# Spacing the typed masks of a graph transformer's second layer in a planned instruction order

## The chip, the cores and the metric

The kernel runs on one core of a Trainium2 chip. The metric is the device time of one execution in microseconds (us). The engines are named as in the profile: PE (TensorE matmul) and PEld (its weight loads), DVE (VectorE), ACT (ScalarE), POOL (GpSimd), SP (SyncE, which here only issues transfers).

## The reference

Two layers of an attention network over a graph with 6250 nodes of 128 values, 200000 edges sorted by destination, 32 edge types, 16 node types and 8 heads; then a linear map, the input added, and a layer norm. What matters of one layer:

```
k, q, v = typed_linear(x, ntype, Wk), ...Wq, ...Wv    # one 128x128 matrix per node type
a   = sum(kT[src, type] * q[dst]) per head            # kT, vT: k and v through one small matrix per edge type
att = softmax of a over the edges of one dst
hag = segment_sum(vT[src, type] * att, dst)
h   = silu(typed_linear(hag, ntype, Wa)) * alpha + x * (1 - alpha)
x   = layer_norm(h) * g + b
```

`typed_linear` multiplies each node's row by the matrix of that node's type. The kernel does it for a group of nodes with 16 masks: mask t holds the transposed rows with all columns zeroed that are not of type t, and 16 matmuls, one per type, add up in one PSUM bank.

## The kernel before

**Stages.** A preparation sorts the nodes by degree and builds, for layer 1, a table in DRAM with one row (key and value, 256 floats) per node and edge type. Each layer then gathers table rows: 49 tiles of 128 nodes, each tile with as many slots as its largest degree needs (1604 slots in all). One gather (line 921, POOL) brings one slot, a row for each of 128 nodes, into a ring buffer in SBUF. In layer 1 the ring has 64 slots, in layer 2 it has 96 (`RINGS`). A gather into a used slot waits until DVE has freed that slot. Layer 1 also builds layer 2's table; layer 2, which the change touches, has gathers, attention and output work only.

**Attention of one tile** (`attend_part`, DVE, in pieces of up to 16 slots): keys times query (L961), sum per head (L963), after all pieces the maximum and the difference (L967 to L972), the exponential on ACT (L974), its sum (L977 to L980), then for each piece values times weights (L988) and their sum (L992). L992 frees the piece's slots.

**Output work of a group** (`behind` and `head`). Tiles form 15 groups: ten of 4 tiles, then groups of 3, 2, 2, 1 and 1. When a group's last tile is done, its sums (`hag`) are transposed on PE; then come 16 masks on DVE (L1072) and 16 matmuls on PE (L1080, tile `av` or `tab`, weights `wa`); one copy on ACT (L1087, `yT`); a transpose back; tanh, skip connection, layer norm, final linear map and second norm; and one scatter per tile on POOL (L1224). In layer 2, two groups can be at this work at once, on two pairs of PSUM banks (`lanes`), taken in turn by a lock that each group gives back near its end.

**Query rows** (`early_rows`, layer 2). One thread goes through groups 2 to 14, loads their layer-1 output from DRAM (`xq`, `tq`), transposes, makes 16 masks and 16 matmuls (weights `wq`), copies (L1087, `qT`), transposes, copies again (`q`) and writes the rows to DRAM, from where a group's tiles fetch them later. It may run any number of groups ahead of the attention.

**Masks.** Both users go through `typed_cols` (L1063). Its `mask` thread makes mask t as soon as the mask buffer is free: with 8 buffers in layer 2 (`XML`), mask t waits for the matmul of mask t-8. The two users share the tag `xm`, so on the chip the 8 buffers go round over the masks of both.

**What sets the order.** `Plan` writes out the order of all instructions before the launch. Every thread yields an engine, a duration and what it needs; `Plan.run` always takes the step that can start first by its own clock; among steps that can start at the same time the lower rank goes first. The ranks here are 1.4 for the masks of the output work ("masks"), 1.6 for attention, 1.8 for the masks of query rows ("early"). On the chip only the order counts: each engine works through its list in that order and waits at an instruction until its semaphores allow it. `LAGS` says that in layer 2 the plan takes the result of any PE work as known 20 us after its end, while gathers run. Scatters are put into POOL's order up to 130 us (`LATE`) after the plan has the rows.

Of the kernel before, what the change touches and what calls it, by code (L numbers as in the profile page):

```python
# [38 lines left out]
P = 128  # L39
# [5 lines left out]
GT = 4  # L45
# [15 lines left out]
XML = (4, 8)  # L61
LAGS = (0.0, 20.0)
XS = (4, 3)
LATE = 130.0
TAB = 512
QUAD = 1.22
GS = 4
# [141 lines left out]
def dve_us(n):  # L209
    return 0.15 + n / 960  # L210


def act_us(n):
    return 0.14 + n / 1200
# [18 lines left out]
def gnn_kernel(ctx: ExitStack, tc: tile.TileContext, x, src, dst, etype, ntype, Wk, Wq, Wv, Wa,  # L233
# [69 lines left out]
    early = ExitStack()  # L303
# [106 lines left out]
    def transposed(t, rows, n, needs):  # L410
        us = yield "PE", Work(n * P), needs
        for j in range(n):
            nc.tensor.transpose(t[:, j * P : (j + 1) * P], rows[:, j], ident)  # L413
        return t, us
# [42 lines left out]
    def table_rows(banks, st, kT, vT, j, bk, bv, needs, free):  # L457

        nodes = slice(j * P, (j + 1) * P)
        width = 2 * HS  # L460
        per = TAB // width
        assert 2 * per == RT
# [3 lines left out]
        for t0 in range(0, RT, per):  # L466
            i = 2 * t0 // RT
            for kv, (cT, blk) in enumerate(((kT, bk), (vT, bv))):
                for g0 in range(0, rows, quad):
                    us = yield "PE", Work(TAB, QUAD if quad > 1 else width / P), [*needs, *emptied[-len(banks):][:quad]]  # L470
                    for g in range(g0, g0 + quad):
# [9 lines left out]
                        def empty(to=st[i][:, :, c0 : c0 + width], tab=tab, done=done, us=us, i=i):  # L481
                            done.us, e = yield ("ACT", "DVE"), (act_us(TAB), dve_us(TAB)), [us, free[i]]
                            (nc.scalar.copy if e == "ACT" else nc.vector.tensor_copy)(  # L483
                                to, tab.rearrange("p (t o) -> p t o", o=width))
# [431 lines left out]
    NG = len(LAST)  # L916
    wqs = []
# [142 lines left out]
            nc.vector.tensor_scalar(low[:, :, 0], low[:, :, 0], float(ROUND), None, op0=ALU.add)  # L1060
            nc.vector.tensor_scalar(low[:, :, 1], low[:, :, 1], float(-ROUND), None, op0=ALU.add)

    def typed_cols(fp, xm_bufs, xT, types, M, maps, needs, rank="masks"):  # L1063

        ready, busy = [When() for _ in range(NT)], [When() for _ in range(NT)]
        masks = {}

        def mask():
            for t in range(NT):
                us = yield "DVE", dve_us(M), [*needs, busy[t - xm_bufs] if t >= xm_bufs else 0.0]  # L1070
                xm = fp.tile([P, GT * P], F32, tag="xm", name="xm", bufs=xm_bufs)
                nc.vector.scalar_tensor_tensor(xm[:, :M], types[:, :M], float(t), xT[:, :M], op0=ALU.is_equal, op1=ALU.mult)  # L1072
                masks[t], ready[t].us = xm, us

        plan.spawn(mask(), RANK[rank])
        for t in range(NT):
            busy[t].us = yield "PE", Work(M * len(maps)), [ready[t]]
            xm = masks.pop(t)
            for w, to in maps:
                nc.tensor.matmul(to[:, :M], w[:, t], xm[:, :M], start=(t == 0), stop=(t == NT - 1))  # L1080
        return busy[-1].us

    def copied4(fp, tag, acc, M, needs, bufs=1):
        us, e = yield ("ACT", "DVE"), (act_us(M), dve_us(M)), needs
        t = fp.tile([P, GT * P], F32, tag=tag, name=tag, bufs=bufs)
        if e == "ACT":
            nc.scalar.copy(t[:, :M], acc[:, :M])  # L1087
        else:
            nc.vector.tensor_copy(t[:, :M], acc[:, :M])
        return t, us  # L1090

    def turned(t, cT, n, needs):
        us = yield "PE", Work(n * P), needs
        for j in range(n):
            nc.tensor.transpose(t[:, j * P : (j + 1) * P], cT[:, j * P : (j + 1) * P], ident)
        return us

    def norm(fp, h, n, bufs=1):
        us = yield "DVE", n * 0.55, ()
        mv = fp.tile([P, GT, 2], F32, tag="mv", name="mv", bufs=bufs)  # L1100
        for j in range(n):
            bst = fp.tile([P, 6], F32, tag="bst", name="bst", bufs=2)
            nc.vector.bn_stats(bst, h[:, j])  # L1103
            nc.vector.bn_aggr(mv[:, j], bst)
        us = yield "ACT", 1.6, [us]
        rs = fp.tile([P, GT], F32, tag="rs", name="rs", bufs=bufs)
        nc.scalar.activation(rs[:, :n], mv[:, :n, 1], AF.Sqrt, bias=eps)  # L1107
        us = yield "DVE", 0.2 + n * dve_us(P), [us]
        nc.vector.reciprocal(rs[:, :n], rs[:, :n])
        for j in range(n):  # L1110
            nc.vector.tensor_scalar(h[:, j], h[:, j], mv[:, j, 0:1], rs[:, j : j + 1], op0=ALU.subtract, op1=ALU.mult)  # L1111
        return us

    def load4(fp, tag, ap, t0, n, bufs):
        t = fp.tile([P, GT, P], F32, tag=tag, name=tag, bufs=bufs)
        nc.sync.dma_start(out=t[:, :n], in_=ap[t0 * P : (t0 + n) * P].rearrange("(j p) d -> p j d", p=P))
        return t

    def behind(fp, layer, i, hag, fetched, needs, weights, wa, at):

        g = LAST[i]
        t0, n = g[0], len(g)
        M = n * P
        lane = lanes[layer * (1 + i % 2)]
        xb, acc, lock = lane
        turn = lock.take()
        xs, types, got = fetched
        xT, us = yield from transposed(xb, hag, n, [*needs, turn])
        at["hag"][i].us = us
        us = yield from typed_cols(fp, XML[layer], xT, types, M, [(wa, acc)], [us, got])  # L1130
        yT, us = yield from copied4(fp, "yT", acc, M, [us], 1 + layer)
        us = yield from turned(xb, yT, n, [us])
        y3 = xb.rearrange("p (j m) -> p j m", j=GT)[:, :n]
        us = yield "ACT", act_us(M) + 1.28, [us] + ([at["h"][i - 1 - layer]] if i > layer else [])
        h = fp.tile([P, GT, P], F32, tag="h", name="h", bufs=1 + layer)[:, :n]
        nc.scalar.activation(h, y3, AF.Tanh, scale=0.5)
        us = yield "DVE", dve_us(M), [us]
        nc.vector.scalar_tensor_tensor(h, h, 1.0, y3, op0=ALU.add, op1=ALU.mult)
        for j, t in enumerate(g):
            xs_us = yield "ACT", 0.3, [got]  # L1140
            nc.scalar.activation(xs[:, j], xs[:, j], AF.Copy, scale=beta[layer][:, t : t + 1])
            us = yield "DVE", dve_us(P), [us, xs_us]
            nc.vector.scalar_tensor_tensor(h[:, j], h[:, j], alpha[layer][:, t : t + 1], xs[:, j], op0=ALU.mult, op1=ALU.add)
        yield from norm(fp, h, n, 1 + layer)
        yield "DVE", dve_us(M), ()
        nc.vector.tensor_tensor(h, h, g_bc[layer][:, None, :].to_broadcast([P, n, P]), op=ALU.mult)  # L1146
        us = yield "DVE", dve_us(M), ()
        nc.vector.tensor_tensor(h, h, b_bc[layer][:, None, :].to_broadcast([P, n, P]), op=ALU.add)  # L1148
        if layer == L - 1:
            yield from head(fp, i, h, lane, [us], at)  # L1150
        else:
            yield from project(fp, i, h, types, weights, [us], at)
# [46 lines left out]
    def head(fp, i, h, lane, needs, at):  # L1199
# [20 lines left out]
        us = yield from norm(fp, o, n, 2)  # L1220
        us = max(us + 1.3, min(us + LATE, at["end"]))
        for j, t in enumerate(g):
# [35 lines left out]
    def attends(fp, layer, ring, pieces, st, weights, wa, pool, landed, freed):  # L1258
# [13 lines left out]
        came = {c: When() for c in ("wq", "wa", "next")}  # L1272
# [55 lines left out]
        def early_rows():  # L1328

            xb, acc, _ = lanes[3]  # L1330
            free, sent = [0.0, 0.0], [0.0, 0.0]
            for i, g in list(enumerate(LAST))[2:]:
                n = len(g)
                got = yield "SP", 0.9, [free[-2]]
                xs = load4(fp, "xq", hid, g[0], n, 1)
                types = fp.tile([P, GT * P], F32, tag="tq", name="tq", bufs=2)
                nc.sync.dma_start(out=types[:, : n * P],
                                  in_=tyrow[ds(g[0] * P, n * P)][None, :].to_broadcast([P, n * P]))
                xT, us = yield from transposed(xb, xs, n, [got + 3.0])
                us = yield from typed_cols(fp, XML[layer], xT, types, n * P, [(wqs[layer], acc)], [us, came["wq"]], "early")  # L1340
                free.append(us)
                qT, us = yield from copied4(fp, "qT", acc, n * P, [us])
                us = yield from turned(xb, qT, n, [us])
                q, us = yield from copied4(fp, "q", xb, n * P, [us, sent[-1]])
                us = yield "SP", 0.4, [us]
                nc.sync.dma_start(out=qrows[g[0] * P : (g[0] + n) * P].rearrange("(j p) d -> p j d", p=P),
                                  in_=q.rearrange("p (j d) -> p j d", d=P)[:, :n])
                sent.append(us + 2.5)
                asked[i].us = us + 2.5
# [20 lines left out]
        for i, g in enumerate(LAST):  # L1370
            if i > 2:
                yield "SP", 0.0, [at["hag"][i - 3]]
            n = len(g)
            hag = fp.tile([P, GT, P], F32, tag="hag", name="hag", bufs=3)
            for j, t in enumerate(g):
# [15 lines left out]
                us = yield "DVE", 0.4 + dve_us(P), ()  # L1391
# [7 lines left out]
    for layer in range(L):  # L1399
        last = layer == L - 1  # L1400
        with tc.tile_pool(name=f"wp{layer}", bufs=1) as wp, tc.tile_pool(name=f"fp{layer}", bufs=1) as fp, \
# [8 lines left out]
            wa = typed_tile(wp, "wa")  # L1410
# [147 lines left out]
```

## Time and profile before

| | |
|---|---|
| median of 3 runs | 6419.52 us (6408.02 to 6420.96) |
| profiled execution | 6422.69 us, its span 6420.9 us |
| busy in the span | PE 2871.1 us, DVE 3917.8 us, ACT 935.9 us, POOL 3427.8 us |
| granted TensorE clock, mean of the span | 0.649 |
| gathers (L921) | 3208, one 1000 ns busy |
| masks of both layers (L1072) | 880, one 589 ns in the mean of all widths |

A row of a list of instructions in order of time reads: start, duration, engine, line, operation, output and inputs, shape, how many were merged, and in brackets the engine's idle time before it with what ended that. "remote" and "issue" as releasers mean that the profile has no instruction of the program at that moment whose end explains the wait.

### The profile page before, as it was taken

What the parts mean: (1) busy time and instruction counts of PE and PEld (TensorE: products, weight loads), DVE (VectorE), ACT (ScalarE), POOL (GpSimd) and SP (SyncE); (2) the same over time, 40 slices, a digit from 0 to 9 for tenths busy, and PEclk for the clock granted to TensorE, in tenths of its full rate; (3) what the DMA queues carried; (4) which work ended last, traced back from release to release, by engine and by line L of the source; (5) the groups of instructions that cost most, each with busy time, mean ns of one, the idle gap of its engine ahead of it and who ended that gap; (6) DMA issues with size and microseconds to landing.
All of it is one profiled execution on the core that took longest, in us unless ns stands there. A gap on an engine that the chain in (4) does not pass through costs nothing. (4 is left out here: it accounts for less than half of the span.)

```text
span 6420.9 us, 36014 instructions
## 1 busy us (share of the span) xinstructions
PE 2871.1 (45%) x8591; PEld 1387.5 (22%) x8599; DVE 3917.8 (61%) x5664; ACT 935.9 (15%) x1921; POOL 3427.8 (53%) x3428
## 2 busy tenths in 40 slices
PE   5887941354555545655655664122232222221112
PEld 4553520121222212221222232010011111110002
DVE  7864637456555655565565563656466666666667
ACT  0333310020211202211111232000000000000001
POOL 4022036555546556555554524766676666767662
PEclk8998975566665566666666776565565565555555
DMA  4696873252525525434444544433333333333331
GB/s 118 264 388 252 338 262 87 74 179 75 186 90 168 178 79 188 168 104 158 157 128 150 181 171 178 117 89 103 103 104 93 98 97 97 99 104 99 94 97 34
DMA packets 323165, 923.16 MB, mean 144 GB/s; under 512 B 82759, under 2 KB 169844, under 8 KB 285312
## 3 DMA queue, kind: packets, MB, share of 16 engines
q0 software_dynamic: 161888, 438.75, 23.6%
q1 hardware_dynamic: 161056, 482.05, 19.9%
q8 instruction: 68, 1.11, 0.1%
q14 instruction: 153, 1.25, 0.1%
HBM read 486.99 MB, written 433.57 MB: 143 GB/s over the span
## 5 line engine op out<-in xcount | busy, mean ns | idle before, releaser
L921 POOL DMA_INDIRECT ring<-table,idx_all x3208 | 3208.5, 1000 | 2498.5 <-issue 2000.9
L1072 DVE SCALAR_TENSOR_TENSOR xm<-types,xb 128x512 f32<-128x512 f32 (+3 forms) x880 | 490.5, 589 | 665.9 <-remote 317.3
L483 ACT COPY st<-tab 128x512 f32<-128x512 f32 x1146 | 613.2, 597 | 1123.6 <-PE tab L474 532.8
L992 DVE TENSOR_REDUCE add<-ring 128x128 f32<-128x2048 f32 (+11 forms) x270 | 745.4, 2761 | 48.4 <-remote 28.6
L474 PE MATMUL tab<-bv,vT 32*128 32x512 f32 x1568 | 478.2, 797 | 172.5 <-issue 89.1
L474 PE MATMUL tab<-bk,kT 32*128 32x512 f32 x1568 | 455.2, 795 | 212.5 <-issue 159.6
L961 DVE TENSOR_TENSOR ring<-ring,sb 128x2048 f32<-128x2048 f32 (+12 forms) x266 | 459.9, 1729 | 143.0 <-DMA ring<-table,idx_all 126.5
L963 DVE TENSOR_REDUCE sb<-ring 128x128 f32<-128x2048 f32 (+11 forms) x270 | 470.7, 1743 | 58.1 <-remote 41.5
L483 DVE COPY st<-tab 128x512 f32<-128x512 f32 x422 | 275.1, 686 | 349.5 <-PE tab L474 176.9
L1080 PE MATMUL av<-xm,wa 128*128 128x512 f32 (+3 forms) x736 | 358.2, 641 | 273.3 <-DVE xm L1072 214.2
L1080 PE MATMUL tab<-xm,wq 128*128 128x512 f32 (+3 forms) x416 | 250.2, 755 | 508.9 <-DVE xm L1072 177.4
L988 DVE TENSOR_TENSOR ring<-ring,sb 128x2048 f32<-128x2048 f32 (+11 forms) x270 | 467.4, 1731 | 0.0
L1080 PE MATMUL av<-xm,wq 128*128 128x512 f32 (+3 forms) x544 | 285.6, 670 | 266.5 <-DVE xm L1072 215.9
L1080 PE MATMUL ak<-xm,wk 128*128 128x512 f32 (+3 forms) x480 | 247.2, 601 | 108.7 <-DVE xm L1072 91.0
L441 PE MATMUL kv<-xm,wk 128*128 128x256 f32 (+1 forms) x800 | 268.1, 419 | 43.4 <-DVE xm L426 42.8
L1234 ACT COPY sb<-qr 128x128 f32<-128x128 f32 x97 | 26.3, 271 | 1691.6 <-DVE sb L963 988.5
L1080 PEld LDWEIGHTS av<-xm,wa 128*128 128x128 f32 x736 | 155.3, 234 | 468.6 <-DVE xm L1072 272.0
L474 PEld LDWEIGHTS tab<-bv,vT 32*128 32x128 f32 x1568 | 170.5, 222 | 373.4 <-issue 178.9
L441 PE MATMUL kv<-xm,wv 128*128 128x256 f32 (+1 forms) x800 | 248.7, 394 | 0.0
L1080 PEld LDWEIGHTS tab<-xm,wq 128*128 128x128 f32 x416 | 105.7, 285 | 642.9 <-DVE xm L1072 217.5
L474 PEld LDWEIGHTS tab<-bk,kT 32*128 32x128 f32 x1568 | 158.6, 221 | 394.8 <-issue 249.9
L1080 PE MATMUL av<-xm,wv 128*128 128x512 f32 (+3 forms) x480 | 234.3, 573 | 0.0
(216 smaller groups left out, 2875.8 us busy)
## 6 DMA issues: line engine op xcount, KB each, us to landing
table<-st SPq DMA_DIRECT2D x196, 1028.0 KB
table<-st SPq DMA_DIRECT2D x98, 2048.0 KB
ring<-table,idx_all POOLq DMA_INDIRECT x3208
state<-init SPq DMA_DIRECT2D x2, 3528.0 KB
state<-state SPq DMA_DIRECT2D x98, 72.0 KB
types<-tyrow SPq DMA_DIRECT2D x20, 256.0 KB
rows<-in_x_dram SPq DMA_DIRECT2D x24, 128.0 KB
types_i<-in_node_type_dram SPq DMA_DIRECT2D x24, 128.0 KB
```

What stands on the lines that cost most here:

```text
L441: nc.tensor.matmul(to, w[:, t], xm, start=False, stop=last_of)
L474: nc.tensor.matmul(tab, cT[here, nodes], blk[here, t0 : t0 + per].rearrange("p t o -> p (t o)"), start=True, stop=True)
L483: (nc.scalar.copy if e == "ACT" else nc.vector.tensor_copy)(to, tab.rearrange("p (t o) -> p t o", o=width))
L921: nc.gpsimd.indirect_dma_start(out=ring[:, place], out_offset=None, in_=tables[layer], in_offset=bass.IndirectOffsetOnAxis(ap=idx[:, s : s ...
L961: nc.vector.tensor_tensor(kk, kk, q[:, None, :].to_broadcast([P, m, P]), op=ALU.mult)
L963: nc.vector.tensor_reduce(sc[:, s0 : s0 + m], kk.rearrange("p s (h d) -> p s h d", h=H), axis=AX.X, op=ALU.add)
L988: nc.vector.tensor_tensor(vv.rearrange("p s (h d) -> p s h d", h=H), vv.rearrange("p s (h d) -> p s h d", h=H), sc[:, s0 : s0 + m, :, None ...
L992: nc.vector.tensor_reduce(add, vv.rearrange("p s c -> p c s"), axis=AX.X, op=ALU.add)
L1072: nc.vector.scalar_tensor_tensor(xm[:, :M], types[:, :M], float(t), xT[:, :M], op0=ALU.is_equal, op1=ALU.mult)
L1080: nc.tensor.matmul(to[:, :M], w[:, t], xm[:, :M], start=(t == 0), stop=(t == NT - 1))
L1234: nc.scalar.copy(q, rows[0][:, j])
```

## The change

`typed_cols` takes one more argument, `pace`. The `mask` thread remembers the planned end of the mask before (`us`) and asks, as one more need, that mask t starts no earlier than `us + pace`. The output work passes `PACE * n / GT` in layer 2 for all but the last three groups (n tiles in the group, GT = 4), else 0. The query rows pass it for every group. `PACE` is 5.5 us: masks of a group of 4 tiles are planned 5.5 us apart from end to start, of 3 tiles 4.125, of 2 tiles 2.75, of 1 tile 1.375. The instructions, their number and their operands stay; their order on the engines' lists may change. Layer 1 passes no pace.

```diff
+PACE = 5.5
...
-    def typed_cols(fp, xm_bufs, xT, types, M, maps, needs, rank="masks"):
+    def typed_cols(fp, xm_bufs, xT, types, M, maps, needs, rank="masks", pace=0.0):
...
         def mask():
+            us = -pace
             for t in range(NT):
-                us = yield "DVE", dve_us(M), [*needs, busy[t - xm_bufs] if t >= xm_bufs else 0.0]
+                us = yield "DVE", dve_us(M), [*needs, us + pace, busy[t - xm_bufs] if t >= xm_bufs else 0.0]
...
-        us = yield from typed_cols(fp, XML[layer], xT, types, M, [(wa, acc)], [us, got])
+        us = yield from typed_cols(fp, XML[layer], xT, types, M, [(wa, acc)], [us, got], "masks",
+                                   PACE * n / GT if layer and i < NG - 3 else 0.0)
...
-                us = yield from typed_cols(fp, XML[layer], xT, types, n * P, [(wqs[layer], acc)], [us, came["wq"]], "early")
+                us = yield from typed_cols(fp, XML[layer], xT, types, n * P, [(wqs[layer], acc)], [us, came["wq"]], "early", PACE * n / GT)
```

## Rows read from the trace of the kernel before

**Rows 1.** Busy time by stretch: from layer 2's first gather to its last, then after.
```profile
3926.00:6294.00 2368.00, 552.41 (x1072) 244.60 (x1072) 1481.80 (x1874) 129.44 (x254) 1641.74 (x1640) 0.57 0.34 101
6294.00:6421.00 127.00, 37.63 (x152) 28.77 (x151) 99.28 (x227) 23.19 (x44) 12.93 (x14) 0.59 0.05 16
```

**Rows 2.** Instructions in order of time, POOL: an undisturbed gather of layer 2.
```profile
4022.13 1.00 POOL L921 DMA_INDIRECT ring<-table,idx_all  x1 [0.30 <-issue]
```

**Rows 3.** Who waited for whom, POOL, 3926 to 6421: total us, times, longest.
```profile
POOL ring L921 <- DVE add L992: 165.0, 16, 17.8
POOL out_dram L1224 <- DVE o L1111: 94.7, 4, 50.6
POOL ring L921 <- DVE rs L1109: 11.7, 1, 11.7
```

**Rows 4.** Groups of masks in layer 2 by shape: busy, mean ns, idle before.
```profile
L1072 DVE SCALAR_TENSOR_TENSOR xm<-tq,tab 128x512 f32<-128x512 f32 x128 | 80.0, 680 | 47.6 <-remote 31.5 <-issue 12.5 <-PE tab L1080 3.6
L1072 DVE SCALAR_TENSOR_TENSOR xm<-types,tab 128x512 f32<-128x512 f32 x80 | 50.6, 682 | 70.3 <-remote 40.3 <-issue 16.6 <-PE tab L1080 13.4
L1072 DVE SCALAR_TENSOR_TENSOR xm<-types,xb 128x512 f32<-128x512 f32 x80 | 50.0, 681 | 33.0 <-remote 23.9 <-issue 5.1 <-PE av L1080 4.0
L1072 DVE SCALAR_TENSOR_TENSOR xm<-tq,tab 128x256 f32<-128x256 f32 x32 | 11.6, 416 | 30.4 <-remote 28.7 <-PE tab L1080 1.7
```

**Rows 5.** DVE in order of time: masks of group 0's output work.
```profile
4227.66 4.87 DVE L1072 SCALAR_TENSOR_TENSOR xm<-types,xb 128x512 f32<-128x512 f32 x8
...
4265.72 0.69 DVE L1072 SCALAR_TENSOR_TENSOR xm<-types,xb 128x512 f32<-128x512 f32 x1 [4.91 <-issue]
4271.32 0.69 DVE L1072 SCALAR_TENSOR_TENSOR xm<-types,xb 128x512 f32<-128x512 f32 x1 [4.91 <-remote]
```

**Rows 6.** PE in order of time: that group's products; two matmul records make one.
```profile
4228.40 8.97 PE L1080 MATMUL av<-xm,wa 128*128 128x512 f32 x16 [12.04 <-issue]
...
4266.46 2.08 PE L1080 MATMUL av<-xm,wa 128*128 128x512 f32 x2 [4.47 <-DVE xm L1072]
```

**Rows 7.** PE in order of time: second half of the first query products.
```profile
3974.45 9.64 PE L1080 MATMUL tab<-xm,wq 128*128 128x512 f32 x16 [10.95 <-issue]
```

**Rows 8.** ACT in order of time: two copies of finished products.
```profile
4014.59 0.59 ACT L1087 COPY qT<-tab 128x512 f32<-128x512 f32 x1 [73.29 <-remote]
...
4594.24 0.58 ACT L1087 COPY yT<-tab 128x512 f32<-128x512 f32 x1 [35.29 <-remote]
```

**Rows 9.** DVE in order of time: the step after an exponential.
```profile
4595.18 0.47 DVE L977 TENSOR_REDUCE den<-sb 128x8 f32<-128x296 f32 x1 [34.48 <-ACT sb L974]
```

**Rows 10.** POOL in order of time: seven gathers that waited for the ring.
```profile
4664.69 0.99 POOL L921 DMA_INDIRECT ring<-table,idx_all  x1 [13.09 <-DVE add L992]
...
4822.25 1.00 POOL L921 DMA_INDIRECT ring<-table,idx_all  x1 [10.45 <-DVE add L992]
...
4884.04 0.99 POOL L921 DMA_INDIRECT ring<-table,idx_all  x1 [14.79 <-DVE add L992]
...
5045.81 0.99 POOL L921 DMA_INDIRECT ring<-table,idx_all  x1 [17.46 <-DVE add L992]
...
5297.00 1.00 POOL L921 DMA_INDIRECT ring<-table,idx_all  x1 [15.55 <-DVE add L992]
...
5446.36 1.00 POOL L921 DMA_INDIRECT ring<-table,idx_all  x1 [17.83 <-DVE add L992]
...
5724.26 1.00 POOL L921 DMA_INDIRECT ring<-table,idx_all  x1 [13.21 <-DVE add L992]
```

**Rows 11.** All masks of query rows in layer 2: ns min/median/max, first and last start.
```profile
L1072 DVE SCALAR_TENSOR_TENSOR xm<-tq,tab x208: 277/678/689, 3953.0 to 5871.8; 128x512 f32<-128x512 f32 x64, 128x256 f32<-128x256 f32 x16, 128x128 f32<-128x128 f32 x16, 128x384 f32<-128x384 f32 x8
```

**Rows 12.** DVE in order of time: first and last masks of group 10's output work.
```profile
6222.65 3.80 DVE L1072 SCALAR_TENSOR_TENSOR xm<-types,xb 128x384 f32<-128x384 f32 x8
...
6246.76 0.99 DVE L1072 SCALAR_TENSOR_TENSOR xm<-types,xb 128x384 f32<-128x384 f32 x2
```

**Rows 13.** DVE in order of time: masks soon after a wait for the ring.
```profile
5600.99 3.18 DVE L1072 SCALAR_TENSOR_TENSOR xm<-types,xb 128x512 f32<-128x512 f32 x5
```

## The prediction

> **What bounds the kernel now.** Read first the busy time by stretch, cut at layer 2's first and last gather [rows 1]: the change passes no pace in layer 1, so nothing before moves. In those 2368 us POOL issues 1640 transfers (1604 gathers, 36 scatters). One takes 1.00 us busy and 0.30 us before the next [rows 2]; 1640 x 1.30 = 2132 us is what gathering alone would need. So 236 us are waiting. The waits by pair come next [rows 3]: 165.0 + 11.7 = 176.7 us of them are gathers that wait for a ring slot that DVE has not freed. The rest, some 59 us, are longer beats and scatters, which no step of this change reaches. DVE, however, is busy only 1482 of the 2368 us [rows 1]. It is late although it has time to spare, so its order and its waits are to be looked at.
>
> The masks grouped by shape [rows 4] show 47.6 + 70.3 + 33.0 + 30.4 = 181.3 us of DVE idle just before masks. What those waits are, the list in order of time tells [rows 5]: after a burst of eight masks in 4.87 us the later ones come one by one at 4265.72, 4271.32 and so on, 5.60 us apart, and DVE does nothing between them. Each wants the buffer of the mask eight before. Eight before the one at 4265.72, counting the masks of query rows between, is the seventh of the burst, and PE was through with the whole burst at 4228.40 + 8.97 = 4237.37 [rows 6]. So DVE waits 28 us and more for a product that is finished. It waits for the news of it, and the news comes one product per 5.60 us. The same is seen elsewhere: PE ends a half group at 3974.45 + 9.64 = 3984.09 [rows 7], and the copy that needs it starts at 4014.59 [rows 8], 30.5 us later or some five and a half such steps. The plan reckons with 20 us. When the copy is that late, ACT stands behind it: at 4594.24 a copy has held ACT for 35.29 us [rows 8], the exponential of a tile stands in ACT's list behind it, and DVE loses 34.48 us [rows 9].
>
> At this point a rule of the Trainium skill is to be weighed: TensorE: Matmul & The Clock Gate, section "The cost: per-tile semaphore tail", says that increments of a semaphore written at the end of matmuls go one after another, and puts about 26 ns on each. By it eight outstanding ones would pass in some 0.2 us (an estimate from that page), the masks would be waiting for PE's work itself, spacing would remove nothing, and the sum below would be 0 saved and 10 us of longer chains, 6430. The trace disagrees by a factor of 200 in size, 5.60 us a step, though not on the order.
>
> **The change part by part.** No instruction is added or removed; DMAs, copies and scatters are the same. What moves is the place of masks in DVE's list, of their products in PE's, and so of all that follows in a group's chain.
>
> *Spacing.* A mask of 512 columns is 0.68 us [rows 4]; with 5.5 us after it one thread asks for a mask every 6.18 us. That is slower than the 5.60 us at which news comes, so one thread alone builds up no queue: its mask t wants news of t-8, 8 x 6.18 = 49 us old, and the copy at the end wants news of a product just done, not of six. Attention pieces fill the 5.5 us. Where both threads run (output work and query rows), 2 masks per 6.18 us are one per 3.1 us, and the queue grows again, by one per 7 us. Narrow groups also stay above: 2 tiles give 2.75 + 0.42 = 3.17 us a mask. These keep part of their waits.
>
> *What it saves.* Only the time that POOL waits counts. Seven long waits follow within 90 us on mask waits or on an exponential held by a late copy [rows 10]: 13.09 + 10.45 + 14.79 + 17.46 + 15.55 + 17.83 + 13.21 = 102.4 us. The others of the 176.7 us (74.3 us) have no such wait before them and stay. Of the seven, those at 5297.00 and 5446.36 (33.4 us) stand behind query masks of groups of 3 and 2 tiles; I take half, 17. Of the other 69.0 us I take two thirds, 46, for the stretches with both threads. Together 63 us; the bounds are 0 (the queue is only moved) and 176.7 (DVE, with 181 us fewer waits, never falls back a ring).
>
> *What it costs.* A chain of 4 tiles now needs 15 x 6.18 = 92.7 us from first to last mask where group 0 was at its thirteenth after 4271 - 4228 = 44 us [rows 5] and the first query group all of them within 3984 - 3953 = 31 [rows 7, 11]. For groups 0 to 9 I count nothing for output chains: two run at once and a group's four tiles at some 33 slots x 1.30 us last 170 us, so the lock comes back in time. For query rows I count nothing either: the last mask is at 5871.8 [rows 11] and no query of the last group is needed before the last gather, 422 us later. If this cover went, 8 groups x 62 us = 496 us of delay would stand against 422, a loss of 74 us. At the end there is no cover: group 10 (3 tiles, the widest near the end) has its masks within 24.6 us now [rows 12] and would have them over 15 x (4.125 + 0.5) = 69 us, 45 us later; group 11 likewise by less. The stretch after the last gather lasts 127 us, of which DVE is busy 99.3 [rows 1]. Work pushed there lengthens it; on the other hand DVE arrives there less far behind, where it now lags by up to a ring of 96 slots. Bounds -30 to +45 us; I take +10, nearer to nothing, as the two pull against each other. POOL meets scatters in its list: the waits of scatters for DVE rows, 94.7 us in four [rows 3], all lie after the last gather, so in the stream they are ahead of need now; a chain 33 us longer leaves most of the 130 us that the plan puts before them. I count 0. PE runs its products one by one, 2.08 us each against 8.97 / 8 = 1.12 in a burst [rows 6]; PE is busy 552 of 2368 us, so that is hidden, except behind the last product of a chain.
>
> *Sum.* -63 + 10 = -53 us on the profiled execution's 6422.7 us: 6370. That execution stands 3.2 us above the median of the runs, so against the median I say 6366 us, 0.8% less.
>
> **The rivals.**
> 1. *Nothing left of the waits.* With masks off DVE's way, copies in time and DVE never a ring behind, all 176.7 us go: 6422.7 - 176.7 + 10 - 3.2 = 6253 us. For it: DVE has 886 us idle in the stretch. Against it: the 74 us that follow on no mask wait.
> 2. *No change.* The number of products stays 448, and at 5.60 us each their news needs 2509 us, more than the 2368 that there are. Then news is the scarce thing, spacing spreads the waits, and POOL still has to stop as often until the queue has drained. For it: right after a wait for the ring the news is quick, five masks pass in 3.18 us without any wait [rows 13], so today's stops are what lets the queue drain. Against it: where PE has been idle, the first products of a burst cost no wait either, so not every one needs a step. Time 6410 to 6430. The rule of the Trainium skill on semaphore increments, if it held, would end here too.
> 3. *Slower: DVE stops at more masks.* The even plan holds for one thread. While both run, masks are asked for at 2 / 6.18 = 0.32 per us and news comes at 1 / 5.60 = 0.18. The difference of 0.145 uses up the 8 buffers after 55 us; from then each further mask stops DVE, with attention steps queued behind it and POOL waiting for what these free. Over a whole 92.7 us the shortfall is 0.145 x 92.7 - 8 = 5.4 masks, 30 us of standing per group, and 300 us for ten groups. Today the mask waits and the held exponential make 181 + 34 = 216 us [rows 4, 9], of which POOL felt 102, or 0.47. Then POOL would wait (300 - 216) x 0.47 = 40 us more: 6420 + 40 + 10 = 6470 us. It turns the sign where the two threads overlap for more than 82 us a group. For it: the query thread took 1919 us for 13 groups [rows 11], so it runs most of the time. Against it: its masks have the lowest rank and come slower than one per 6.18 us.
>
> **How the numbers follow.** The forecast (part of the waits goes, 6300 to 6406) 0.48, rival 1 0.15, rival 2 0.15, rival 3 0.22. This kernel's runs differ by 13 us, 0.2%, about what can be told from no change: faster below 6407, slower above 6432. Faster has the forecast and rival 1, 0.63; same 0.15; slower 0.22. The range takes in rival 1's time and most of the way to rival 3's: 6255 to 6460. The forecast's own range is 6300 to 6406.
>
> **What would show it.** Right: in layer 2 the bursts of eight masks of 512 columns are gone, and single ones stand between ring instructions some 6 us apart; DVE's idle before 512-column masks falls from 151 us to under 60; no wait of 20 us or more for ACT before L977; POOL's waits on `add` L992 fall from 165 to about 100 us; the beat between undisturbed gathers stays 1.30 us. Wrong: mask waits of 4.9 us remain in strings (rival 2), POOL's waits fall under 40 us (rival 1), or DVE's idle before masks grows beyond 181 us, with the waits inside the attention of a tile (rival 3). The 10 us at the end are wrong if the stretch after the last gather leaves 97 to 172 us. The saving would be mis-sized rather than wrong if the mask waits go and POOL's do not follow.

## The result, and the profile after

The changed kernel is slower by a little: 6449.99 us in the median of 6 runs (6440.59 to 6453.41) against 6406.20 us (6395.61 to 6420.96, 6 runs of the kernel before), ratio 1.0063 with a 95% interval of [1.0048, 1.0079]. That is clear of noise and under 1%. (The ratios here are those on record; they differ by up to 0.001 from the quotients of the medians.) Forecast were 6366 us, and a chance of 0.22 for slower. The profiled execution took 6449.19 us, 26.5 more than the profiled one of before.

One thing must be known to read the later numbers. In the first two sets of runs the kernel before took 6406 and 6421 us in the median, and news of PE products (what tells DVE and ACT that a product is done) came one per 5.60 us, as the forecast had it. I call this late news. In the last four sets the same kernel took some 5240 us and that delay was absent; I call this prompt news. No set showed both. The second set ran on chip 15, the four with prompt news on chips 10, 7, 6 and 3, and the first set's chip is not on record. Whether the delay belongs to a chip or to some other condition of a set can't be told, as no chip on record was met twice. Each ratio stands against the kernel before in the same set of runs.

The stretches come first, as in [rows 1], cut at the first and last gather of each layer. A line has the stretch, its length, the busy us and the number of instructions of PE, PEld, DVE, ACT and POOL, then the granted clock, the DMA share and GB/s. The kernel before, layer 1 and the gap between the layers:

```profile
879.00:3788.00 2909.00, 1470.64 (x3290) 618.03 (x3291) 1688.61 (x2114) 476.07 (x1031) 1602.36 (x1604) 0.64 0.44 141
3788.00:3926.00 138.00, 100.11 (x517) 67.21 (x516) 81.95 (x196) 56.77 (x116) 0.40 (x2) 0.79 0.45 188
```

and the changed kernel, of which the last two lines answer to [rows 1]:

```profile
877.00:3689.00 2812.00, 1472.73 (x3213) 601.04 (x3213) 1663.87 (x2073) 476.70 (x1028) 1605.95 (x1604) 0.65 0.46 146
3689.00:3854.00 165.00, 117.72 (x594) 79.79 (x593) 92.37 (x228) 61.52 (x126) 0.10 (x1) 0.83 0.39 162
...
3854.00:6321.00 2467.00, 628.46 (x999) 224.88 (x1000) 1476.37 (x1855) 131.46 (x254) 1644.77 (x1643) 0.55 0.34 97
6321.00:6447.00 126.00, 58.12 (x225) 44.13 (x225) 98.94 (x245) 21.08 (x44) 9.90 (x10) 0.62 0.07 19
```

Layer 1, of which I had said that it does not move, is 97 us shorter, the gap between the layers 27 longer, layer 2's gather stretch 99 longer, and the end about the same. POOL's own work in that stretch is nearly equal (1641.74 and 1644.77 us), so the 99 us are waits. Who waited for whom on POOL, layer 2 of the changed kernel (answers to [rows 3], where `add` had 165.0 us in 16 waits, none over 17.8):

```profile
POOL ring L922 <- DVE add L993: 214.6, 10, 39.6
POOL out_dram L1227 <- DVE o L1113: 85.4, 5, 46.6
```

Few and long stops: from one gather's start to the next, beyond the usual 1.30 us, there are seven of 24 to 41 us (the last of them has four scatters in it). The first ends at 5252 us; the 966 gathers of layer 2 before it have none over 5 us. The masks by shape, layer 2 (answers to [rows 4]):

```profile
L1074 DVE SCALAR_TENSOR_TENSOR xm<-tq,tab 128x512 f32<-128x512 f32 x128 | 85.1, 680 | 87.6 <-remote 49.1 <-issue 21.8 <-PE av L1082 9.8
L1074 DVE SCALAR_TENSOR_TENSOR xm<-types,xb 128x512 f32<-128x512 f32 x80 | 54.3, 678 | 13.3 <-issue 10.9 <-PE av L1082 1.6 <-PE tab L1082 0.8
L1074 DVE SCALAR_TENSOR_TENSOR xm<-types,tab 128x512 f32<-128x512 f32 x80 | 54.2, 679 | 20.5 <-issue 12.9 <-remote 5.9 <-PE tab L1082 1.7
L1074 DVE SCALAR_TENSOR_TENSOR xm<-tq,tab 128x256 f32<-128x256 f32 x32 | 12.9, 414 | 43.6 <-remote 18.7 <-issue 12.8 <-PE tab L1082 6.9
```

The output masks' waits fell from 103.3 to 33.8 us, those of the query masks rose from 78.0 to 131.2. One stop in detail. The issues of SP (start, duration) show a group's query rows written (`qrows<-q`), then loaded (`qr<-qrows`) by the attention that needs them; the time between is called slack below. Group 8, before:

```profile
5067.64 0.38 SPq L1346 DMA_DIRECT2D qrows<-q  x1
...
5666.29 0.70 SPq L1116 DMA_DIRECT2D qr<-qrows  x1
```

and after:

```profile
5647.48 0.38 SPq L1349 DMA_DIRECT2D qrows<-q  x1
...
5649.91 0.37 SPq L1118 DMA_DIRECT2D qr<-qrows  x1
```

599 us of slack became 2.4. In the changed kernel the slack is 109 us for group 2, 29 for group 3, and under 5 for all from group 4 on. The PE products of group 8's query rows show why: the first four come 22 to 30 us apart, then they fall together. Three of these four:

```profile
5512.75 1.91 PE L1082 MATMUL tab<-xm,wq 128*128 128x512 f32 x2
...
5539.47 2.07 PE L1082 MATMUL tab<-xm,wq 128*128 128x512 f32 x2 [1.14 <-issue]
...
5561.20 2.07 PE L1082 MATMUL tab<-xm,wq 128*128 128x512 f32 x2 [6.33 <-DVE xm L1074]
```

`attends` loads the next group's rows before it starts the last tile of its own group (`load_rows` ahead of `attend`), so the plan puts nothing of that tile into DVE's list until those rows are planned as written. On the chip DVE, done with the tile before, meets all remaining masks in one string:

```profile
5558.59 0.68 DVE L1074 SCALAR_TENSOR_TENSOR xm<-tq,tab 128x512 f32<-128x512 f32 x1
5559.19 0.68 DVE L1074 SCALAR_TENSOR_TENSOR xm<-types,xb 128x512 f32<-128x512 f32 x1
...
5575.17 0.69 DVE L1074 SCALAR_TENSOR_TENSOR xm<-tq,tab 128x512 f32<-128x512 f32 x1 [4.91 <-PE av L1082]
5580.77 0.69 DVE L1074 SCALAR_TENSOR_TENSOR xm<-tq,tab 128x512 f32<-128x512 f32 x1 [4.91 <-PE av L1082]
...
5638.13 0.69 DVE L1141 SCALAR_TENSOR_TENSOR h<-h,xb 128x512 f32<-128x512 f32 x1 [34.27 <-ACT h L1139]
```

and POOL, whose ring is full, waits for DVE:

```profile
5665.31 1.00 POOL L922 DMA_INDIRECT ring<-table,idx_all  x1 [38.88 <-DVE add L993]
```

The even distance existed on the plan's clock only. Where the plan had no other DVE work, the masks lie side by side in the list, and a DVE that is behind the plan runs them as a burst.

### The profile page after: what moved, and what is told of

Same layout as the page of the kernel before. It is cut to its first block, busy times and chain, and to the rows that moved or that the text cites. A ratio compares the mean times of both kernels' runs of the same rounds, so it can differ in the third digit from the quotient of the medians.

```text
span 6447.0 us, 36021 instructions
## 1 busy us (share of the span) xinstructions
PE 2986.0 (46%) x8591; PEld 1377.1 (21%) x8599; DVE 3896.7 (60%) x5656; ACT 941.2 (15%) x1927; POOL 3431.0 (53%) x3428
## 5 line engine op out<-in xcount | busy, mean ns | idle before, releaser
L1082 PE MATMUL av<-xm,wa 128*128 128x512 f32 (+3 forms) x736 | 422.2, 710 | 452.2 <-DVE xm L1074 242.8
L1082 PE MATMUL tab<-xm,wq 128*128 128x512 f32 (+3 forms) x416 | 278.4, 782 | 558.6 <-DVE xm L1074 222.0
L475 PE MATMUL tab<-bv,vT 32*128 32x512 f32 x1568 | 453.9, 777 | 138.4 <-issue 85.1
L1082 PE MATMUL av<-xm,wq 128*128 128x512 f32 (+3 forms) x544 | 299.6, 691 | 217.9 <-DVE xm L1074 106.5
L1082 PE MATMUL tab<-xm,wa 128*128 128x512 f32 (+2 forms) x224 | 168.0, 856 | 334.4 <-DVE xm L1074 157.0
```

The source lines that it names most:

```text
L475: nc.tensor.matmul(tab, cT[here, nodes], blk[here, t0 : t0 + per].rearrange("p t o -> p (t o)"), start=True, stop=True)
```

## Experiments

Cut at the same gathers, all in us (one profiled execution each; "ratio" is of the timed runs, against the kernel before of the same set). "Edge" means the new need between two masks at a pace of 0. "Slack" is the least from write to load of the query rows of groups 2 to 9.

| kernel | layer 1 gathers | gap | layer 2 gathers | last gather to end | slack | ratio |
|---|---|---|---|---|---|---|
| before, late news | 2908.1 | 138.6 | 2367.5 | 127.7 | 344 | 1 |
| changed | 2810.3 | 166.2 | 2466.7 | 125.9 | 2 | 1.0063 [1.0048, 1.0079] |
| e1 layer 2 only | 2894.4 | 138.5 | 2460.3 | 124.8 | 2 | 1.0162 [1.0148, 1.0176] |
| e2 layer 1 only | 2805.9 | 166.8 | 2361.5 | 126.5 | 343 | 0.9902 [0.9879, 0.9924] |
| e3 output spaced | 2819.5 | 164.7 | 2341.7 | 131.5 | 292 | 0.9901 [0.9887, 0.9915] |
| e4 query spaced | 2826.2 | 165.6 | 2486.5 | 129.5 | 2 | 1.0093 [1.0076, 1.0109] |
| before, prompt news (f1) | 2092.4 | 114.8 | 2141.1 | 60.1 | 296 | 1 |
| r1 changed | 2096.3 | 136.9 | 2153.8 | 53.2 | 3 | 1.0059 [1.0045, 1.0072] |
| r2 layer 1 only | 2095.2 | 136.7 | 2141.5 | 59.6 | 296 | 1.0045 [1.0031, 1.0058] |
| r3 query rank 1.5 | 2098.1 | 138.3 | 2140.2 | 48.3 | 160 | 1.0027 [1.0017, 1.0038] |
| r4 query pace 2 | 2097.3 | 137.2 | 2141.9 | 54.7 | 168 | 1.0037 [1.0023, 1.0050] |
| f2 layer 2, rank 1.5 | 2092.9 | 114.6 | 2139.8 | 48.8 | 160 | 0.9977 [0.9968, 0.9986] |
| f3 edge in 10 groups | 2098.5 | 123.2 | 2140.9 | 49.1 | 160 | 0.9996 [0.9987, 1.0005] |
| g3 query only, rank 1.5 | 2093.8 | 113.7 | 2142.7 | 57.6 | 157 | 0.9998 [0.9989, 1.0007] |
| e7 layer 1 pace 2 | 2296.5 | 209.5 | 2142.8 | 59.4 | 296 | 1.0581 [1.0566, 1.0595] |
| e9 layer 1 rank 1.7 | 2106.1 | 188.5 | 2141.5 | 60.4 | 296 | 1.0164 [1.0150, 1.0178] |

**The two layers apart (e1, e2).** A pace of 0 is not the old list of needs: `us + pace` is the planned end of the mask before, to which the planner adds 0.12 us (`HOP_US`) for every step. So the second mask can start 0.12 us later than an attention step that is ready, and loses the place that its rank of 1.4 gave it. In layer 1's DVE order a string becomes an alternation. Before:

```
L1072 xm<-types,xb x2
L961  ring<-ring,sb
L963  sb<-ring
L967  sb<-sb,pen_all
```

After:

```
L1074 xm<-types,xb
L962  ring<-ring,sb
L1074 xm<-types,xb
L964  sb<-ring
L1074 xm<-types,xb
L968  sb<-sb,pen_all
```

In the changed kernel's trace 264 masks stand alone between other steps from layer 1's first gather to layer 2's, against 50 before. In the experiments a pace of `None` gives the old needs:

```diff
+us = yield "DVE", dve_us(M), [*needs, 0.0 if pace is None else us + pace, busy...]
e1: -rank="masks", pace=0.0):   +rank="masks", pace=None):     # layer 2 as changed
e2: -PACE * n / GT              +None                          # both users of layer 2
```

> Layer 1 gets back its old list of needs (no planned edge from mask to mask), layer 2 is spaced as in the changed kernel. In the two traces layer 2's first gather came at 3925.8 us before and at 3854.3 after, although layer 1 passes no pace. Theory A (two separate effects: with a pace of 0 each mask still needs the end of the mask before plus 0.12 us, which splits the strings of masks in layer 1 and saves 71 us; the spacing itself loses 99 us in layer 2 because query rows come just in time): first gather of layer 2 near 3926, from there to the last gather near 2467, total 6450 + 71 = 6521, range 6495 to 6540. Theory B (the early start of layer 2 has nothing to do with the edge, layer 1 only varies from run to run or from compile to compile): total near 6450. Theory C (news of products is what is scarce, and a later start of layer 2 is made good later): 6450 to 6480.

> Layer 1 as in the changed kernel (needs with the edge of 0.12 us, pace 0), layer 2 exactly as before (no edge, no pace). Theory A: layer 2's first gather near 3854, from there to the last gather near 2367 as before, total 6406 - 71 = 6335, range 6320 to 6355. Theory B: 6400 to 6415. Theory C: between, 6340 to 6380, as layer 2 would meet other stops.

Medians of 6523.6 and 6353.56 us against 6421.42 us before. Theory A holds, theories B and C fall: e1 has layer 1 and the gap of before and the layer 2 of the changed kernel, e2 the reverse. (e2's total alone would not tell A from C, whose ranges overlap there; e1's total and the stretches do.) In e1's trace DVE's list is that of the kernel before, instruction for instruction, up to layer 2's first query mask, so the edge is what changes the order of layer 1. The first gather of layer 2 with the idle time before it, e1:

```profile
3912.18 0.99 POOL L922 DMA_INDIRECT ring<-table,idx_all  x1 [137.48 <-issue]
```

and e2:

```profile
3851.68 1.00 POOL L922 DMA_INDIRECT ring<-table,idx_all  x1 [165.80 <-issue]
```

The change is two unlike ones: its side effect in layer 1 gains about 1%, its purpose in layer 2 loses 1.6%. How the alternation saves 98 us there is not shown. DVE's idle time before layer 1's masks, while gathers run, falls from 609.0 to 543.9 us, but it is 582.5 in e1, without the edge, and 575.6 to 583.3 in e2, e3 and e4, with it, so it does not go with the gain. What does go with it is DVE's idle time before the first step of attention after all pieces of a tile (L967 before, L968 after), in these lines before and after:

```profile
L967 DVE TENSOR_TENSOR sb<-sb,pen_all 128x256 f32<-128x256 f32 (+19 forms) x48 | 20.9, 435 | 136.2 <-ACT sb L1234 64.7 <-issue 31.9 <-ACT st L483 23.4
...
L968 DVE TENSOR_TENSOR sb<-sb,pen_all 128x256 f32<-128x256 f32 (+19 forms) x48 | 20.8, 434 | 64.6 <-ACT sb L1237 59.8 <-issue 4.3
```

It is 131.6 us in e1 and 64.4 to 68.3 in e2, e3 and e4. Why that wait shrinks, and whether it is the whole gain, was not traced.

**The two users apart (e3, e4).** Layer 1 with the edge; in e3 `early_rows` passes `None`, in e4 `behind` does.

> As the changed kernel, but only the output work of layer 2 is spaced; the query rows make their masks as soon as a buffer is free, as before. Theory A (the loss of layer 2 is the query rows alone, which from group 5 on are written 2.5 us before they are loaded, where 370 to 600 us lay between before): the slack of the query rows is over 200 us for all groups again, the seven stops of POOL of 20 to 42 us are gone, layer 2 from first to last gather 2310 to 2380, total 6280 to 6345. Theory D (my third rival: two threads ask for masks faster than news comes, so any spacing of output work makes DVE stand longer): stops of POOL remain, first to last gather over 2430, total above 6400.

> As the changed kernel, but only the query rows of layer 2 are spaced; the output work makes its masks as soon as a buffer is free. Theory A: slack of the query rows 2 to 5 us from group 5 or 6 on, POOL stops once per group by 25 to 45 us, first to last gather 2430 to 2490, total 6415 to 6470. Theory D: with one spaced thread no queue is built, total 6300 to 6350.

6354.83 and 6482.50 us. With only the query rows spaced, their slack is gone and seven stops of 30 to 42 us return; with only the output work spaced the slack stays at 292 us and more, and the longest stop is 21 us. So the spacing of the query rows makes the loss. That it does so because the rows come late is read from the stop above; no run with late news had query rows that were spaced and in time. But e3 saves nothing either: its median is that of e2 (6353.56), its gather stretch 20 us shorter in one profile, with runs that spread over 25 to 46 us. Where the gain went is seen by shape. In e2, unspaced, masks and the step after tanh:

```profile
L1074 DVE SCALAR_TENSOR_TENSOR xm<-types,tab 128x512 f32<-128x512 f32 x80 | 50.6, 684 | 69.5 <-remote 51.8 <-PE tab L1082 10.8 <-issue 6.9
L1074 DVE SCALAR_TENSOR_TENSOR xm<-types,xb 128x512 f32<-128x512 f32 x80 | 49.7, 681 | 34.0 <-issue 16.1 <-remote 14.0 <-PE av L1082 3.8
...
L1141 DVE SCALAR_TENSOR_TENSOR h<-h,xb 128x512 f32<-128x512 f32 x5 | 3.4, 687 | 24.1 <-issue 24.1
L1141 DVE SCALAR_TENSOR_TENSOR h<-h,tab 128x512 f32<-128x512 f32 x5 | 3.4, 678 | 0.0
```

In e3, spaced:

```profile
L1074 DVE SCALAR_TENSOR_TENSOR xm<-types,xb 128x512 f32<-128x512 f32 x80 | 54.0, 680 | 21.7 <-issue 12.9 <-remote 8.7
L1074 DVE SCALAR_TENSOR_TENSOR xm<-types,tab 128x512 f32<-128x512 f32 x80 | 54.0, 679 | 42.9 <-remote 29.8 <-issue 12.9
...
L1141 DVE SCALAR_TENSOR_TENSOR h<-h,tab 128x512 f32<-128x512 f32 x5 | 3.4, 684 | 53.4 <-issue 53.4
L1141 DVE SCALAR_TENSOR_TENSOR h<-h,xb 128x512 f32<-128x512 f32 x5 | 3.4, 684 | 26.2 <-issue 26.2
```

The idle time before output masks falls by 38.9 us, that before the step after tanh grows by 55.5. The wait left the mask for the end of the same chain of output work.

**Query rows in time (e5, e8, r1 to r4).** e5 and r3 are one kernel: the changed one with `early=1.5` in `RANK`. e8 and r4 are one: output work `None`, query pace `2.0 * n / GT`. r1 is the changed kernel, r2 is e2.

> As the changed kernel, both users spaced by 5.5 us, but the masks of query rows get rank 1.5 instead of 1.8, so that at the same planned time they go ahead of an attention step. Theory A (after a spaced mask the query thread loses its turn to attention, and gets one mask into each gap of the plan, one per 20 to 28 us): with the rank its masks follow each other by some 6 to 11 us, 16 of them in 100 to 180 us, the slack of the query rows is over 150 us for most groups, and the seven stops of POOL of 24 to 41 us are gone. What my forecast counted on, the gain of spacing without late query rows, is then seen here: layer 2 from first to last gather 2361 - 63 = 2300 and total near 6290 if it holds; 2330 to 2365 and 6330 to 6360 if spacing saves little, as the run with spaced output work alone says. Theory E (the query rows are late because of the 8 buffers or the news of products, not by their turn): slack stays under 10 us, total 6430 to 6480.

> As the changed kernel, but the output work of layer 2 is not spaced and the query masks are planned 2.0 us apart (for 4 tiles) instead of 5.5, at their old rank 1.8. A piece of 16 slots takes 20.8 us to gather and DVE some 10 us, so the plan has gaps of about 10 us. Theory A (one spaced mask per gap at 5.5): three or four masks per gap, 16 masks in 85 to 130 us, slack of the query rows over 100 us, no stops of 24 us or more, total 6325 to 6370. Theory E (spacing as such makes the query thread late): slack under 20 us from group 5 on, total above 6430.

> The changed kernel once more, beside the three below. In the last four runs the kernel before took 5238 us and not 6406 to 6421: there POOL never stopped in layer 2 and no mask waited for news of a product, so that chip does not show the delay of 5.60 us per product on which everything so far rests. If this call meets the delay again: ratio 1.005 to 1.008 and about 6450 us, as at first. If it does not: nothing is there for layer 1's edge to save, the query rows still come 2 to 5 us before they are loaded, since that is a matter of the plan's order, but DVE does not stand at masks while it waits, and ratio 1.00 to 1.01.

> Layer 1 with the edge of 0.12 us from mask to mask, layer 2 as before. With the delay of news: ratio near 0.990 as in the first measurement. Without it: the edge has no stop of POOL to save in layer 1; the changed order at the end of layer 1 may move the start of layer 2 by some 20 us either way: ratio 0.997 to 1.005.

> Both users spaced by 5.5 us, query masks at rank 1.5. Where news was prompt this was 1.0031 of before, with 119 to 211 us of slack for the query rows of groups 2 to 12. With the delay of news, theory A: slack over 150 us, none of the stops of 24 us and more, total 6290 if spacing then saves the 63 us of my forecast, 6330 to 6360 if it saves little. Theory E (late for the buffers or the news, not for their turn): slack under 10 us, 6430 to 6480.

> Output work of layer 2 not spaced, query masks planned 2.0 us apart at rank 1.8. Where news was prompt: 1.0042 of before, slack 155 us and more up to group 11. With the delay of news, theory A: slack over 100 us, no stops of 24 us or more, total 6325 to 6370. Theory E: slack under 20 us from group 5 on, above 6430.

Medians, with before at 5237.85 us (e5, e8) and 5239.81 us (r1 to r4): e5 5255.50, e8 5261.94, r1 5271.92, r2 5265.17, r3 5254.42, r4 5260.43. All of these met prompt news, so the totals that were expected for late news are untested. What the order alone decides is settled for theory A: going earlier by rank (1.5 instead of 1.8) or a smaller pace gives the query rows 155 us and more of slack up to group 10, while the changed kernel has 3 us from group 4 on here too (r1). The 16 query masks of group 5 take 191 us from first to last in r1 and 109 in r3. With prompt news lateness costs little: 12 us of gather stretch (r1 against r2), nearly all of it one stop of 10 us. So late rows alone don't make the seven stops: under late news DVE, meeting a string of masks, also waits 4.91 us at mask after mask. Spacing is worth about that where its rows are in time: r3 is 10.7 us under r2, all of it after the last gather.

**Layer 1's edge (e7, e9, f1, f3).** e7: pace 2.0 in layer 1. e9: no edge, rank 1.7 for its masks. f1 is the kernel before, for its trace. f3: as f2 below, with the edge where `i < NG - 5`.

> Layer 2 as before; in layer 1 all masks are planned 2.0 us apart instead of the 0.12 us that a pace of 0 gives. Theory A1 (what helps layer 1 is that one step of other work comes between two masks): a step of attention takes 0.3 to 3.8 us, so little changes against 0.12 us; last gather of layer 1 at 3670 to 3710, total 6330 to 6365. Theory F (more distance is better, since each mask waits for news of the product four before): last gather of layer 1 under 3650, total under 6310. Theory G (the chain of 16 masks becomes the bound): last gather of layer 1 above 3760, total above 6410.

> Layer 2 as before; in layer 1 no edge between masks, but the masks get rank 1.7 instead of 1.4, behind attention (1.6). Theory A1 (alternating is what helps): here a mask only comes when no attention step can start, and when it comes several come together as before, so it is not as good as the edge: total above 6375, and above 6421 if the output chains of layer 1 starve as the query rows did in layer 2. Theory H (it only matters that attention goes ahead of masks): last gather of layer 1 3670 to 3710, total 6330 to 6365.

> The kernel before itself, for its trace beside the runs of this call. If news of products is prompt here (about 5240 us): no stop of POOL over 6 us in either layer, layer 2 from first to last gather near 2141, and from layer 1's last gather to layer 2's first some 110 to 115 us, where the kernels with the edge in layer 1 took 136.7 us; tail near 57 us. If news is delayed (about 6420 us): 138 us at that place and 2367 us in layer 2, as in the first trace.

> As the run before this one, but with the edge of 0.12 us in layer 1 for the first ten groups; the last five groups have no edge. Theory A2 (the edge saves stops of POOL in layer 1 where news is late, and costs 24 to 28 us after layer 1's last gather because the alternation leaves masks over for the end; without it for the last groups that cost goes): with prompt news the gap between the layers is 110 to 120 us and the total 5226 to 5236; with delayed news 6421 - 99 - (0 to 63) = 6260 to 6325. Theory I (the left-over is made earlier, in the wide groups): the gap stays at 130 us and more, total with prompt news 5245 to 5260.

5543.93, 5327.19, 5241.02 (one run) and 5237.73 us. With prompt news there is no stop in layer 1 to save, so e7 and e9 say only what more distance costs, and theories F and H stay untested where they matter. e7 makes POOL stop six times in layer 1, 195 us in all (theory G's direction; that its longer chains are the cause was not traced); e9 leaves more work over for the gap, which takes 188 us. The gap is DVE, PE and table stores that remain when the last gather of layer 1 is out. The gap in f1 (columns as above):

```profile
2923.00:3038.00 115.00, 79.42 (x426) 55.14 (x422) 66.90 (x165) 46.65 (x93) 1.12 (x2) 0.80 0.46 189
```

in r2, with the edge everywhere:

```profile
2926.00:3062.00 136.00, 94.54 (x485) 61.74 (x477) 79.13 (x184) 54.27 (x111) 0.45 (x1) 0.81 0.46 191
```

and in f3:

```profile
2928.00:3051.00 123.00, 84.55 (x450) 57.98 (x450) 73.00 (x180) 51.97 (x102) 0.82 (x2) 0.80 0.48 198
```

So the edge costs 22 us here and 28 with late news, and more instructions are left over with it (485 against 426 on PE). Taking it from the last five groups recovers 13.6 of the 21.9 us. Neither theory's range is met: the gap of 123.2 us is 3 above A2's 120 and below theory I's 130.

**Both users spaced in layer 2 alone (f2, g1, g2, g3).** f2 and g1: layer 1 with the old needs, both users of layer 2 spaced, `early=1.5`. g2 is e5 again; g3 spaces the query rows alone, at rank 1.5.

> Layer 1 exactly as before (no edge), in layer 2 both users spaced by 5.5 us with the query masks at rank 1.5, so that query rows come in time: what the change was meant to be, without its two side effects. With prompt news: the stretch from layer 2's first to its last gather stays at 2141, the tail is 46 instead of 57 us, so 5229 us, ratio 0.998. With delayed news, theory A: slack of the query rows over 150 us, no stops of 24 us and more; total 6421 - 63 = 6358 if spacing saves what I forecast, 6390 to 6420 if it saves little. Theory E: slack under 10 us, total above 6500.

> Layer 1 as before, both users of layer 2 spaced by 5.5 us, query masks at rank 1.5. With prompt news it was 0.9977 of before. With delayed news: query rows in time (slack over 150 us for groups 2 to 9, theory A) and ratio 0.990 (6421 - 63) if spacing saves what I forecast, 0.995 to 1.000 if little; theory E: slack under 10 us, ratio 1.012 and more.

> The same layer 2 with the edge of 0.12 us in layer 1. With prompt news it was 1.003. With delayed news: ratio 0.990 (the edge alone, as measured) less whatever spacing saves in layer 2, 0.980 to 0.990; theory E: 1.003.

> Layer 1 as before; in layer 2 only the query masks are spaced, at rank 1.5, and the output masks come as soon as a buffer is free. With prompt news: if the tail of 46 us instead of 57 comes from the output work's spacing, tail 57 and ratio 1.000; if from the query rows', tail 46 to 51 and ratio 0.998. With delayed news: slack over 100 us (theory A), ratio 0.995 to 1.003.

f2 5227.15 us against 5239.86; g1 5226.64, g2 5255.20 and g3 5238.56 against 5239.60, g1's ratio 0.9976 [0.9967, 0.9985], g2's 1.0031 [1.0020, 1.0043]. With prompt news f2 is 0.23% faster than before and 0.85% faster than the changed kernel (r1, another set of runs); nearly all of it lies after the last gather (48.8 against 60.1 us). It needs the output work's spacing, since g3, without it, has 57.6 there; whether that spacing does it alone was not run, and why the end is shorter was not traced. Whether f2 gains where news is late was not seen. There e2 is the fastest together with e3.

## Why the prediction was wrong

- The time lies inside the wide range of 6255 to 6460 us only because that took in most of the way to the third rival; the forecast's own range, 6300 to 6406, and its sign were wrong.
- "The change passes no pace in layer 1, so nothing before moves" failed. It was read from the argument and not from the need that the argument goes into. It is worth 98 us less in layer 1's gathers and 28 more in the gap; without it the loss is 1.6% (e1).
- "For query rows I count nothing" is the step that decided the sign. The cover of 422 us was taken as one reserve at the end, but each group's rows are needed before the last tile of the group ahead, every 200 us or so. And the 92.7 us of a chain were priced by the spacing alone: a query mask of rank 1.8 that has waited out its distance finds DVE given to attention and takes the next gap. Its 16 masks took 158, 211, 169 and 234 us in groups 2 to 5, where 25, 44, 123 and 70 were before. The prediction's own price for that cover gone, a loss of 74 us, is not far from the 99 us measured, but by luck: it adds all delays up to the end, where the loss came group by group. It got no chance of its own.
- The saving of 63 us failed in size at least for the output half: 20 us of the gather stretch in the profile of e3, none in its median. The waits moved on to the step after tanh, which is near to what the second rival said of scarce news. Both users spaced with rows in time were not seen under late news.
- Right: the stretch after the last gather is within 97 to 172 us (126, though 2 less than before and not the 10 more of the forecast); no wait of 20 us for an exponential is left ([rows 9] had 34.48; the longest now is 2.7, below); the beat is still 1.30 us. Scatters ahead of the last gather, priced at 0, waited some 20 us for the late output rows of group 9.

```profile
DVE den L978 <- ACT sb L975: 24.8, 17, 2.7
```

- Of the expected signs, the idle before masks of 512 columns fell from 151 to 121 us and not under 60, and POOL's waits on `add` rose to 214.6.
- The third rival had the sign, and its time, 6470, is 20 us off, as far as the top of the second's range, 6430. Its mechanism was not seen: DVE's idle before the four shapes fell from 181.3 to 165.0 us and did not grow, and the loss came from spacing one thread alone (e4), not from two spaced together.

## What to carry to other kernels

A new need with a neutral value is still a need: before pricing a change to a planned order, compare the two orders everywhere, also in stages that it is not meant for. A low-rank thread that feeds a later stage is judged by the time between its write and the load that wants it, group by group; spacing its steps can cost it a turn at each, here up to 30 us for a distance of 5.5. A delay that a forecast rests on should be seen in more than one set of runs.

## What the runs showed of the hardware that was not expected

The delay of PE's news is not always there. In [rows 7] and [rows 8] a copy starts 30.5 us after the end of 16 matmul records. In f1, the same program, PE:

```profile
3086.51 9.37 PE L1080 MATMUL tab<-xm,wq 128*128 128x512 f32 x16 [11.20 <-DVE xm L1072]
```

and ACT:

```profile
3095.91 0.59 ACT L1087 COPY qT<-tab 128x512 f32<-128x512 f32 x1 [43.51 <-PE tab L1080]
```

The copy comes 0.03 us after 3086.51 + 9.37 = 3095.88, while gathers run at the same beat:

```profile
3134.25 1.00 POOL L921 DMA_INDIRECT ring<-table,idx_all  x1 [0.30 <-issue]
```

and masks of layer 2 no longer wait:

```profile
L1072 DVE SCALAR_TENSOR_TENSOR xm<-tq,tab 128x512 f32<-128x512 f32 x128 | 79.0, 680 | 0.0
```

The Trainium skill, TensorE: Matmul & The Clock Gate, section "The cost: per-tile semaphore tail", gives some 26 ns per increment, measured there on small matmuls packed side by side. The 0.03 us of f1 are of that order of size; the 5.60 us a step of the first trace are some 200 times as much. The kernel before takes about 1180 us less of 6420 with prompt news; that the delay makes all of this difference was not shown. Its condition was not found: the durations of masks (680 ns at 512 columns) and gathers (1.00 us) are alike in both.
